# Four transformer layers in one kernel: the list scheduler orders the instructions by its other timing model

## The chip, the core and the metric

The kernel runs on one core of a Trainium2 chip. The metric is the device time of one execution in microseconds (us); lower is better. A core has five engines that run side by side, each through its own list of instructions in order, and that wait for one another through semaphores: TensorE (PE; its weight loads are shown as PEld), VectorE (DVE), ScalarE (ACT), GpSimd (POOL) and SyncE (SP), which here issues DMAs.

## The reference

The input `x` has 32 sequences of 64 tokens with 256 features; `ctx_2048`, of the same shape, is the context. Four layers follow one another, all in float32:

```python
x = L0(x, ctx, self_mask, cross_mask)  # self attention, cross attention, MLP (16 heads of 16)
x = L1(x, ctx)   # linear recurrence over the tokens: s = k*v + w*s per head, then a gated feed-forward
x = L2(x, ctx, ctx)  # two cross attentions with 16 heads of 128 and a bias key and value, then an MLP
x = L3(x, ctx, key_mask)  # cross attention (16 heads of 16) and an MLP
```

Every attention is `softmax(q k^T * scale) v`, every sublayer has a layer norm ahead of it and adds to its residual.

## The kernel before

The 2048 tokens are cut into four groups (`g` = 0 to 3) of 512 tokens, eight sequences each. Activations lie feature by feature as 128x512 tiles, two for 256 features. A layer of a group is a Python generator (`layer0` to `layer3`) that yields between steps, and `weave` interleaves a main generator with lighter ones at fixed rates: while layer 2 of group 0 is written, layer 1 of group 1 and layer 0 of group 2 are written between its steps, and so on. `keep` is a further light one: it computes the keys and values of layer 2's first attention ahead (tiles `k2p_f`, `v2p_f`, evicted to `fk` on ScalarE, L928, and `fv` on VectorE, L937), stores them in DRAM and loads them again later (`kd`, `vd`).

This text order isn't the order that the engines run. When the `TileContext` closes, a list scheduler takes all instructions with their dependencies and goes through them by a timing model: whatever the model holds ready, with the earliest place in the text first, is put next on its engine. The semaphores are set for that order. Buffers rotate within pools (`ps1`, four PSUM banks for single tiles; `ps2`, two pairs of banks), and an instruction that fills a buffer waits for the last reader of what was there.

Names that the rest uses:

- `norm` (L174 to L194): statistics and `xn` (L180) on VectorE, transposes `nt` on TensorE (L190), then `y` or `h`, feature by feature: half 0 on VectorE (L192), half 1 on ScalarE (L194).
- `linear` (L165): 128x512 matmuls, two for each output tile; `q2p`, `k2p`, `qp`, `kp`, `h` (the MLPs) and others. `token_linear` (L328): 128x256 matmuls, tiles `al`.
- `attn16`, the attention of layers 0 and 3: scores `sp` (L269, 32 rows of the array), softmax on VectorE and ScalarE, the product with the reciprocal sum on GpSimd (L276), transposes `tp` (L286), value products `pv` (L295), `oT` (L299).
- `bias_attn`, the attention of layer 2: scores `s2p` (L788, 64 columns of the array), softmax, transposes `tp2` (L802), value products `pv2` (L817, shown as `pv`), evictions `o` (L827 on ScalarE, L828 on VectorE), then `al_o`.
- the recurrence of layer 1, `states`: `vj` on TensorE (L550), a product (L559) and two scans (L565) on VectorE, a product on GpSimd (L566), `op` (L588) on TensorE.

The value products of layer 2 write two banks, one for each sequence of a pair (`b2`), and go through them in turn; `half` are rows of the array, `rows` its columns:

```python
for m in range(2):
    rows = slice(64 * m, 64 * m + 64)
    hc = (2 * pp + h2) * P + 64 * m
    for b2 in range(2):
        half = slice(64 * b2, 64 * b2 + 64)
        PE.matmul(
            pv[b2][rows, to : to + S], vals[bp][half, hc : hc + 64],
            pt[half, bp, h2 * S : (h2 + 1) * S], start=True, stop=True,
        )
```

Of the kernel before, what the change touches and what calls it, by code (L numbers as in the profile page):

```python
# [1072 lines left out]
def build(arrays):  # L1073
    import concourse.bacc as bacc

    nc = bacc.Bacc("TRN2", target_bir_lowering=False, num_devices=1)
    args = [
        nc.dram_tensor(f"in_{n}", a.shape, mybir.dt.from_np(a.dtype), kind="ExternalInput").ap()
        for n, a in arrays.items()
    ]  # L1080
    args.append(nc.dram_tensor("out_0", (P, G, TT, D), F32, kind="ExternalOutput").ap())
    with tile.TileContext(nc) as tc:
        kernel(tc, *args)
    return nc

# [12 lines left out]
```

## Time and profile before

| | before |
|---|---|
| median of 3 runs (lowest to highest) | 2216.41 us (2216.34 to 2218.59) |
| the profiled execution | 2216.37 us, span 2214.6 us |
| PE busy | 2057.4 us, 93% of the span |
| DVE busy | 1097.3 us, 50% |
| ACT busy | 632.9 us, 29% |
| POOL busy | 597.5 us, 27% |
| DMA | 197.25 MB, mean 89 GB/s |

The span is the time from the first to the last instruction that the hardware profiler recorded. Busy is the time in which an engine had at least one instruction running. A float32 matmul has two records in the trace, a transpose one. Tile names are shown without their numbers. "x <- y" in a list of waits means that x stood still until y was done. Clock is the share of TensorE's full clock that was granted.

### The profile page before, as it was taken

How to read it: one execution, taken by the hardware profiler on the slowest of the kernel's cores; microseconds unless marked ns; L12 is line 12 of the kernel's file. 1: busy time of each engine (PE TensorE's matmuls, PEld its weight loads, DVE VectorE, ACT ScalarE, POOL GpSimd, SP SyncE). 2: the span in 40 equal slices, each digit the busy share in tenths (PEclk: the TensorE clock that was granted, in tenths of full speed). 3: DMA queues.
4: the chain of work that ended last, by engine and by line, in shares of the span. 5: the costliest groups of instructions: out<-in, count | busy, mean ns of one | idle time of the engine just before them, and what ended most of it. 6: DMA issues, size and time to landing. Idle time of an engine off the chain costs nothing. (4 is left out here: it accounts for less than half of the span.)

```text
span 2214.6 us, 36273 instructions
## 1 busy us (share of the span) xinstructions
PE 2057.4 (93%) x15264; PEld 1242.9 (56%) x15264; DVE 1097.3 (50%) x1885; ACT 632.9 (29%) x1000; POOL 597.5 (27%) x498
## 2 busy tenths in 40 slices
PE   5889998899999898999997999999999999999998
PEld 3445444354555465755554656555566767565665
DVE  3552557423655636335556463266564355424661
ACT  1222322132321322232313132322233233222442
POOL 2331344213423314214324141233221112200220
PEclk9999998999999999999998999999999999999999
DMA  7233231226412212243121123341213342213010
GB/s 247 93 106 118 93 110 57 93 101 229 141 49 64 66 41 63 92 132 109 55 62 58 42 79 96 121 134 44 86 45 108 100 152 69 78 51 94 22 41 20
DMA packets 79794, 197.25 MB, mean 89 GB/s; under 512 B 9616, under 2 KB 14352, under 8 KB 79632
## 3 DMA queue, kind: packets, MB, share of 16 engines
q1 hardware_dynamic: 77472, 191.88, 27.1%
q8 instruction: 121, 1.98, 0.4%
q0 software_dynamic: 576, 2.10, 0.3%
q10 hardware_dynamic: 1584, 0.95, 0.2%
q14 instruction: 41, 0.34, 0.1%
HBM read 158.98 MB, written 35.91 MB: 88 GB/s over the span
## 5 line engine op out<-in xcount | busy, mean ns | idle before, releaser
L165 PE MATMUL q2p<-h,w 128*128 128x512 f32 x512 | 245.4, 612 | 6.8 <-DMA w<-in_wts 3.2
L328 PE MATMUL al_o<-w,o 128*128 128x256 f32 x1024 | 235.1, 388 | 11.7 <-DVE o L828 10.7
L328 PEld LDWEIGHTS al_o<-w,o 128*128 128x128 f32 x1024 | 196.6, 194 | 52.6 <-issue 20.6
L778 ACT ACTIVATE q<-q2p,vt 128x512 f32<-128x512 f32 x128 | 87.5, 685 | 278.9 <-PE q2p L165 275.7
L165 PEld LDWEIGHTS q2p<-h,w 128*128 128x128 f32 x512 | 94.9, 193 | 123.6 <-issue 105.5
L796 POOL TENSOR_TENSOR pn<-s,sm 128x512 f32<-128x512 f32 x64 | 69.7, 1091 | 285.2 <-DVE sm L209 198.2
L165 PE MATMUL k2p_f<-c,w 128*128 128x512 f32 x256 | 131.2, 634 | 4.9 <-DMA w<-in_wts 2.8
L726 PE MATMUL v2p_f<-w,c 128*128 128x512 f32 x256 | 122.4, 601 | 0.0
L165 PE MATMUL k2p<-c,w 128*128 128x512 f32 x256 | 120.7, 597 | 0.0
L726 PE MATMUL v2p<-w,c 128*128 128x512 f32 x256 | 119.1, 609 | 1.1 <-DVE k L764 1.1
L566 POOL TENSOR_TENSOR a<-a,r 128x1024 f32<-128x1024 f32 x32 | 76.1, 2378 | 109.8 <-DVE a L565 96.4
L937 DVE TENSOR_TENSOR fv<-v2p_f,vb 128x512 f32<-128x512 f32 x64 | 43.9, 687 | 124.7 <-PE v2p_f L726 124.7
L928 ACT ACTIVATE fk<-k2p_f,vt 128x512 f32<-128x512 f32 x64 | 43.9, 686 | 175.4 <-PE k2p_f L165 146.8
L341 DVE TENSOR_TENSOR x<-al_o,x 128x512 f32<-128x512 f32 x64 | 43.6, 683 | 101.2 <-PE al_o L328 101.2
L828 DVE TENSOR_SCALAR o<-pv,vt 128x256 f32<-128x256 f32 x128 | 55.8, 473 | 76.6 <-PE pv L817 76.4
L764 DVE TENSOR_SCALAR k<-k2p,vt 128x512 f32<-128x512 f32 x64 | 47.4, 743 | 91.4 <-PE k2p L165 91.4
L788 PEld LDWEIGHTS s2p<-k,q 128*64 128x64 f32 x2048 | 67.7, 138 | 40.8 <-issue 29.7
L817 PEld LDWEIGHTS pv<-pt,v 64*64 64x64 f32 x4096 | 72.8, 140 | 26.6 <-issue 18.4
L565 DVE TENSOR_TENSOR_SCAN a<-ws,a 128x512 f32<-128x512 f32 x64 | 85.4, 1368 | 1.7
L726 PEld LDWEIGHTS v2p_f<-w,c 128*128 128x128 f32 x256 | 49.6, 195 | 63.5 <-issue 61.3
L817 PE MATMUL pv<-pt,v 64*64 64x64 f32 x4096 | 81.7, 226 | 3.2 <-issue 1.5
L165 PEld LDWEIGHTS k2p<-c,w 128*128 128x128 f32 x256 | 49.4, 193 | 62.1 <-issue 59.4
(305 smaller groups left out, 3678.5 us busy)
## 6 DMA issues: line engine op xcount, KB each, us to landing
w<-in_wts SPq DMA_DIRECT2D x200, 512.0 KB, 3.7
kd<-fk SPq DMA_DIRECT2D x64, 260.0 KB, 2.1
k<-kd SPq DMA_DIRECT2D x64, 260.0 KB, 3.8
vd<-fv SPq DMA_DIRECT2D x64, 256.0 KB, 2.0
v<-vd SPq DMA_DIRECT2D x64, 256.0 KB, 4.5
vb<-in_vrow SPq DMA_DIRECT2D x20, 256.0 KB, 4.1
vs<-in_vrow SPq DMA_DIRECT2D x20, 256.0 KB, 3.4
c<-in_cT POOLq DMA_DIRECT2D x4, 512.0 KB, 11.6
```

Of the source, the lines that this page charges most:

```text
L165: PE.matmul(ps, w[:, o : o + cols], y[:, kc, :], start=(kc == 0), stop=(kc == NC - 1))
L328: PE.matmul(ps[:, a, :], y[kc][:, i * P : (i + 1) * P], wk[:, o : o + D], start=(kc == 0), stop=(kc == k - 1),)
L565: V.tensor_tensor_scan(a[:, i, :], ws[:, c, :], a[:, i, :], 0.0, ALU.mult, ALU.add)
L566: PL.tensor_tensor(a, a, r[:, c : c + 1, :].to_broadcast([P, 2, GT]), ALU.mult)
L726: PE.matmul(ps, cs[g][:, kc, bp * P : (bp + 1) * P], wv[:, 512 * kc : 512 * kc + 512], start=(kc == 0), stop=(kc == NC - 1),)
L764: V.tensor_scalar_add(k[:, :, :S], bt(ps), vec(f"L2_xattn_bk{a}", hd))
L778: A.activation(q, ps, AF.Identity, bias=vec(f"L2_xattn_bq{a}", hd))
L788: PE.matmul(sp[64 * h2 : 64 * h2 + 64, b // 4, (b % 4) * (S + 1) : (b % 4 + 1) * (S + 1)], qs[h2][:, b * S : (b + 1) * S], ks[h2][:, b, :] ...
L796: PL.tensor_tensor(pn, s[:, :, :S], rc.unsqueeze(2).to_broadcast([P, GB, S]), ALU.mult)
L817: PE.matmul(pv[b2][rows, to : to + S], vals[bp][half, hc : hc + 64], pt[half, bp, h2 * S : (h2 + 1) * S], start=True, stop=True,)
L828: V.tensor_scalar_add(ov[:, :, 1, :], src[1], bv)
L928: A.activation(k[:, :, :S], bt(ps), AF.Identity, bias=vec("L2_xattn_bk1", hd))
```

## The change

The context that holds the scheduler is opened with an option: the scheduler takes a timing model that follows queues and semaphores in place of its default one. Nothing in the text of the kernel changes, so the engines get the same instructions with the same operands, in another order, with semaphores set for it.

```diff
@@ -1079,7 +1079,7 @@
     args.append(nc.dram_tensor("out_0", (P, G, TT, D), F32, kind="ExternalOutput").ap())
-    with tile.TileContext(nc) as tc:
+    with tile.TileContext(nc, schedule_with_timeline_sim=True) as tc:
         tile_layers_kernel(tc, *args)
     return nc
```

## The prediction

> **What bounds the kernel now.** I read the page's busy rows first, then its slices, the waits, the timeline of single places, and last the instruction orders of the two built programs side by side.
>
> ```profile
> span 2214.6 us, 36273 instructions
> PE 2057.4 (93%) x15264; PEld 1242.9 (56%) x15264; DVE 1097.3 (50%) x1885; ACT 632.9 (29%) x1000; POOL 597.5 (27%) x498
> PE   5889998899999898999997999999999999999998
> PEclk9999998999999999999998999999999999999999
> ```
>
> TensorE is the bound: 2057.4 of 2214.6 us, so all idle time together is 157.2 us. A reordering can gain at most that, and it can lose in two ways: new idle time, or TensorE instructions that take longer beside other neighbours. Where the idle time sits is in the waits:
>
> ```profile
> PE tp_a L286 <- POOL s_a L276: 20.4, 6, 5.9
> PE nt_a L190 <- DVE xn_a L180: 19.8, 1, 19.8
> PE tp_b L286 <- POOL s_b L276: 13.9, 6, 7.1
> PE al_o L328 <- DVE o L828: 10.7, 5, 3.2
> PE sp_a L269 <- DVE s L205: 10.4, 4, 4.7
> ...
> PE tp_b L286 <- DVE fv L937: 5.5, 1, 5.5
> ```
>
> The columns are total us, times, longest. The 19.8 is the start, before any data is there. The rest are short waits in which an attention of layer 0 or 2 follows its softmax chain through VectorE and GpSimd.
>
> **What moves.** Each engine has the same instructions in both programs: 8112 matmuls, 1885 on VectorE. TensorE's are shifted by 4.1 places in the mean, VectorE's by 1.2, SyncE's DMAs by 0.3. So this is no new plan, but many small swaps. I price the TensorE swaps, then the stalls, then the rest.
>
> **1. The value products (pv, L817), +17.7 us.** One group is 32 matmuls of 64x64 into two PSUM banks (`b2`); the two banks use the two row halves of the array, `m` its two column halves. The source alternates them, and in the program of before 130 neighbouring pairs within the groups stay in one bank; in the changed one 736 do: it starts bank 0 with 8 or 9 matmuls, then bank 1, and alternates only after that. The trace of before has both patterns:
>
> ```profile
> 572.75 1.16 PE L817 MATMUL pv<-pt,v 64*64 64x64 f32 x64
> 573.84 1.13 PE L480 MATMUL mp<-t,w 32*128 32x512 f32 x4
> 574.89 3.70 PE L165 MATMUL q2p<-h,w 128*128 128x512 f32 x8
> 578.52 1.16 PE L817 MATMUL pv<-pt,v 64*64 64x64 f32 x64
> ...
> 1935.56 1.15 PE L788 MATMUL s2p<-k,q 128*64 128x65 f32 x32
> 1936.64 1.98 PE L165 MATMUL h_j<-y_j,w 128*128 128x512 f32 x4
> 1938.56 1.15 PE L788 MATMUL s2p<-k,q 128*64 128x65 f32 x32
> ...
> 1943.61 1.15 PE L817 MATMUL pv<-pt,v 64*64 64x64 f32 x32
> 1945.44 1.15 PE L817 MATMUL pv<-pt,v 64*64 64x64 f32 x32 [0.68 <-ACT hm_j L349]
> ```
>
> Each row is start, duration, and a count of records; a matmul of this type has two. Alternating, 64 records take 1.16 us; at 1943.61 one bank alone takes 1.15 us for 32. Take off the last record's own 0.218 us (median of the pv rows): 0.94/64 = 14.7 ns a record against 0.93/32 = 29.1, hence 14.6 ns more, 29.2 ns a matmul. 736 - 130 = 606 pairs x 29.2 ns = 17.7 us. Bounds: zero where bank 1 is really still held (then before would have waited), and 26.5 if the whole group at 788 is the price (it took 2.38 us with 28 such pairs: 1.22/28 = 44 ns, of which 0.14 is a wait). Sixty of the 64 groups of before show no wait inside, so I take 17.7.
>
> **2. Visits of small matmuls between long ones, +14 us.** Going from a 128-row, 128-column matmul (transposes apart) to one on a part of the array happens 124 times before and 180 times after, the way back 135 and 188: 54 more visits. Splits such as one score matmul (s2p, L788) ahead of q2p and the other 15 behind it make them. The rows above price one: eight records of q2p take 578.52 - 574.89 = 3.63 us to the next start, four of h_j between two small groups 1938.56 - 1936.64 = 1.92, and 3.63 - 1.92 = 1.71 for four more; so a visit costs the long ones 0.21. The small group pays its own start: the 32 s2p records hold TensorE for 1936.64 - 1935.56 = 1.08 us, while (1.15 - 0.225)/31 = 29.8 ns a record in the midst of the run (0.225 is the mean of one in the page) makes 0.95; 0.13 more. Ends 54 x 0.21 = 11 and 54 x 0.34 = 18; I take 14, nearer the first, since some visits only move. [...]
>
> **3. The stalls, -5 us, the least certain term.** Where the order around a wait is the same, it stays: tp_a at 772 and 1208 (5.9 each), sp_a at 749 and 1183 (4.5 and 4.7), the last nt_j (3.8), the start. At the start two VectorE instructions that wait for mc move behind the first norm, but the next instruction, k2p_f, waits for its weight until 24.8 us anyway: nothing. What can go is the stage where layer 1 of group 0 runs beside the cross attention of group 1:
>
> ```profile
> 280.00:320.00 40.00, 38.41 (x247) 19.91 (x246) 18.77 (x34) 12.22 (x19) 17.43 (x19) 1.00 0.33 108
> 320.00:360.00 40.00, 37.72 (x204) 17.52 (x206) 29.38 (x35) 8.98 (x17) 15.38 (x13) 0.91 0.19 68
> 360.00:400.00 40.00, 26.36 (x161) 13.30 (x154) 34.72 (x33) 8.94 (x14) 24.11 (x14) 0.83 0.14 50
> ```
>
> (Windows by stage: length, then busy PE, PEld, DVE, ACT, POOL, granted clock, DMA share, GB/s.) From 320 to 400 TensorE idles 2.3 + 13.6 = 15.9 us while VectorE is full, and from 280 to 320 VectorE is half empty. The changed order brings the state products (vj, L550) and their VectorE work (L559 1.20 us, two scans L565 of 1.37: 3.9 us a state) of four states forward. But it puts them ahead of the norm's xn_b (L180) and y_b (L192), on which qp_b and all of that attention wait: 14.5 us of state work now stands in front of y_b on VectorE that stood behind it. So a wait of up to some 11 us (14.5 less the 3.6 us state that ran there anyhow) opens at 318 for up to 15.9 that closes later. The middle of +11 and -15.9 is -2.5; the late stretch also runs at a granted clock of 0.83, which on its 26.4 busy us is 0.17 x 26.4 = 4.5 more to win, so I take -7. Elsewhere: al_o behind its evictions at 604 and 1039 (3.2 and 3.1) gets 8 and 6 more matmuls in front, -4; tp_a at 57 (5.8) gets 16 score matmuls in front, -1.5. New or longer: al_d behind og (2.7 twice) loses 1.4 us of cover twice, op behind its state 1 us twice, q2p behind h at 1554 3.0: +7.8. Sum -4.7.
>
> **4. The rest, nothing.** ScalarE gets 57 table loads for 64; at 1.283 us a row that is 9.0 us of an engine that is 29% busy, and no TensorE wait above 2.7 us ends on ScalarE: 0, bounds 0 and -9.0. [...] On SyncE's queue the latest-moved loads are k for s2p_110 behind eight others; before, these were all issued by 550.4 and s2p needs k at 567.6, with 4 us from issue to landing: hidden by 13 us; without that cover it would cost the 4 us.
>
> **Sum.** 17.7 + 14 = 31.7 us more on TensorE; it idles 7% of the time and part falls into waits that are there, so I count nine tenths, 28.5. Less 5: +23.5. The profiled execution took 2216.37 us (span 2214.6 and 1.8 around it), the median of the runs is 2216.41, so the two can be used alike: 2239.9, forecast 2240.
>
> **Rivals.**
> *A, faster: the stalls close.* Mechanism: the new order takes VectorE's state work out of the full stretch 360 to 400. It decides if y_b is not held up at 318: then -15.9 - 4.5 there, -5.5 for al_o and tp_a, and the products' bank order costs nothing because bank 1 is still held; against 14 for visits: 2216 - 26 + 14 = 2204. For it speaks the half-empty VectorE at 280 to 320; against it the order on VectorE and the pv rows without waits. 0.18.
> *B, much slower: VectorE blocks.* State work now also stands ahead of pv evictions (L828: 3.9 us at 602 and 1037, 7.6 at 1464) and of y_b (up to 11). If VectorE runs these first, TensorE waits at al_o and qp_b: 11 + 3.9 + 3.9 + 7.6 = 26 on top of 28.5: 2271. Against it: these state products come earlier on TensorE too. 0.19.
> *C, no difference.* The timing model changes little, mean shift 4 places; gains of A's 26 meet the 28.5: 2218. Against it the 606 pairs, whose price is measured. 0.08.
>
> **Chances.** The forecast has 0.55. Under 0.2% (4.4 us) this kernel's measurement cannot tell from none. Faster 0.18 (A), same 0.08 (C), slower 0.74 (forecast and B). The range leaves out the lower half of A and the upper half of B, one in ten on each side: 2208 to 2268.
>
> **What would show it.** Right: PE busy near 2085 to 2090; pv rows in the timeline with 1.4 to 1.5 us a group for 1.16; PE idle about 150. Step 2 is wrong if PE busy rises by no more than pv's share, step 3 if a wait of nt_b or qp_b on DVE at 318 is missing or the 360 to 400 stretch still has 13 us idle. The forecast as a whole is wrong if PE busy stays at 2057 or if idle falls below 125.

## The result and the profile after

The changed kernel takes 2290.31 us (median of 4 runs, 2286.05 to 2292.28) beside 2216.38 us before: the ratio is 1.033, 95% interval 1.031 to 1.035. The forecast was 2240, its range ended at 2268. The side was right, the size was not: +74 us for +23.5.

The page of the changed kernel, its span and busy row:

```profile
span 2288.5 us, 36279 instructions
...
PE 2105.9 (92%) x15264; PEld 1268.5 (55%) x15264; DVE 1114.6 (49%) x1885; ACT 624.4 (27%) x993; POOL 600.8 (26%) x498
```

The span grew by 73.9 us: TensorE is busy 48.5 us longer and idles 25.4 us longer (182.6 for 157.2). Of the busy time a part is clock. The clock records of the trace know two values, 1.0 and 0.5; laid over TensorE's busy time, 108.9 us ran at half clock before and 145.1 after. At half clock the work goes half as fast (records of 128x512 matmuls start 0.85 us apart at 1558 us of the kernel before and 0.43 us apart at 1561, when the clock is full again), so half of the difference, 18.1 us, is put down as time lost. So 73.9 = 25.4 idle + 18.1 half clock + 30.4 that is left, TensorE's work that takes longer at the same clock; runs 1 and 2 show what makes most of it. Terms 1 and 2 of the prediction, 31.7 together, meant the last number. Term 3, -5, meant the first two, 43.5.

The waits of TensorE in the changed kernel (total, times, longest, in us):

```profile
PE tp_a L286 <- POOL s_a L276: 14.0, 6, 6.0
...
PE al_d L328 <- POOL og L619: 9.5, 2, 4.7
PE qp_b L165 <- issue: 9.3, 1, 9.3
PE al_o L328 <- DVE o L828: 9.2, 3, 4.5
...
PE tp L802 <- POOL pn L796: 6.8, 3, 3.4
```

Some of the old waits did get shorter: tp_a 20.4 to 14.0, tp_b 13.9 to 7.4. In their place stand waits that the list of before hardly has or doesn't have: qp_b, nt_b (8.8 us in all), a longer al_d, tp behind pn, dwp behind xm on GpSimd (4.2 us). The largest are in the stage that the prediction priced at -7 (windows as before: length, busy PE, PEld, DVE, ACT, POOL, clock, DMA share, GB/s):

```profile
320.00:360.00 40.00, 24.71 (x77) 11.66 (x76) 28.05 (x29) 5.52 (x11) 16.24 (x10) 0.79 0.20 66
360.00:400.00 40.00, 31.85 (x197) 14.71 (x195) 29.93 (x31) 9.93 (x16) 20.00 (x12) 0.87 0.12 44
```

From 320 to 400 TensorE idles 15.3 + 8.1 = 23.4 us, where it idled 15.9 before. These are equal windows of time, not equal work. The instructions that the kernel before ran from 281.7 to 400 us run here from 285.3 to 423.8, 20.2 us longer: the idle time in them rises from 17.5 to 34.3 us, the busy time at half clock from 14.9 to 23.2. VectorE's timeline there shows why (start, duration):

```profile
323.63 6.66 DVE L565 TENSOR_TENSOR_SCAN a<-ws,a 128x512 f32<-128x512 f32 x4
330.21 3.38 DVE L180 TENSOR_SCALAR xn_b<-x,mv_b,rs_b 128x256 f32<-128x256 f32 x4
...
336.35 6.66 DVE L565 TENSOR_TENSOR_SCAN a<-ws,a 128x512 f32<-128x512 f32 x4
342.93 0.78 DVE L192 TENSOR_SCALAR y_b<-nt_b,vt 128x512 f32<-128x512 f32 x1
```

And TensorE's:

```profile
330.74 0.66 PE L190 MATMUL nt_b<-ct,xn_b 128*128 128x128 f32 x2 [4.43 <-DVE xn_b L180]
...
343.81 3.57 PE L165 MATMUL qp_b<-y_b,w 128*128 128x512 f32 x4 [9.26 <-issue]
347.22 1.88 PE L165 MATMUL kp_b<-c,w 128*128 128x512 f32 x4
```

Two states (two scans L565 each) stand in front of xn_b and two more in front of y_b. The three waits, 4.43, 1.60 (in the row that is left out) and 9.26, make 15.3 us, where the prediction had "up to some 11". The list calls the longest one "issue"; the start of qp_b at 343.81, right behind the end of y_b at 343.71, tells who it waited for. Its four records then take 3.57 us, at half clock up to 347.1; kp_b's four behind it take 1.88.

TensorE's own work in the changed kernel, with a cut score group and a group of value products:

```profile
597.90 0.33 PE L788 MATMUL s2p<-k,q 128*64 128x65 f32 x2
598.16 1.13 PE L480 MATMUL mp<-t,w 32*128 32x512 f32 x4
599.22 1.15 PE L788 MATMUL s2p<-k,q 128*64 128x65 f32 x30
...
604.37 1.55 PE L817 MATMUL pv<-pt,v 64*64 64x64 f32 x64
```

One score matmul goes ahead of mp and the other 15 follow it; a value group takes 1.55 us for 1.16.

### The profile page after: what moved, and what is told of

Same layout as the page of the kernel before. It is cut to its first block, busy times and chain, and to the rows that moved or that the text cites. A ratio compares the mean times of both kernels' runs of the same rounds, so it can differ in the third digit from the quotient of the medians.

```text
span 2288.5 us, 36279 instructions
## 1 busy us (share of the span) xinstructions
PE 2105.9 (92%) x15264; PEld 1268.5 (55%) x15264; DVE 1114.6 (49%) x1885; ACT 624.4 (27%) x993; POOL 600.8 (26%) x498
## 5 line engine op out<-in xcount | busy, mean ns | idle before, releaser
L566 POOL TENSOR_TENSOR a<-a,r 128x1024 f32<-128x1024 f32 x32 | 76.8, 2400 | 120.7 <-DVE a L565 97.9
L817 PEld LDWEIGHTS pv<-pt,v 64*64 64x64 f32 x4096 | 87.7, 138 | 28.0 <-issue 21.8
L817 PE MATMUL pv<-pt,v 64*64 64x64 f32 x4096 | 96.7, 226 | 3.4 <-issue 1.5
L200 DVE TENSOR_REDUCE mx<-s2p 128x8 f32<-128x520 f32 x64 | 44.2, 691 | 107.0 <-PE s2p L788 106.4
L828 DVE TENSOR_SCALAR o<-pv,vt 128x256 f32<-128x256 f32 x128 | 55.2, 473 | 79.7 <-PE pv L817 79.4
L565 DVE TENSOR_TENSOR_SCAN a<-ws,a 128x512 f32<-128x512 f32 x64 | 91.6, 1474 | 1.5
L788 PE MATMUL s2p<-k,q 128*64 128x65 f32 x2048 | 86.0, 226 | 3.2 <-DVE xm L482 1.3
```

What stands on the lines that cost most here:

```text
L200: V.tensor_reduce(mx, src, AX.X, ALU.max)
L565: V.tensor_tensor_scan(a[:, i, :], ws[:, c, :], a[:, i, :], 0.0, ALU.mult, ALU.add)
L566: PL.tensor_tensor(a, a, r[:, c : c + 1, :].to_broadcast([P, 2, GT]), ALU.mult)
L788: PE.matmul(sp[64 * h2 : 64 * h2 + 64, b // 4, (b % 4) * (S + 1) : (b % 4 + 1) * (S + 1)], qs[h2][:, b * S : (b + 1) * S], ks[h2][:, b, :] ...
L817: PE.matmul(pv[b2][rows, to : to + S], vals[bp][half, hc : hc + 64], pt[half, bp, h2 * S : (h2 + 1) * S], start=True, stop=True,)
L828: V.tensor_scalar_add(ov[:, :, 1, :], src[1], bv)
```

## The experiments

In each kernel below every engine's order is written out: at the end of the program text a chain of dependencies without semaphores ties each instruction to the one that shall stand ahead of it on its engine. With the orders of the changed kernel so pinned, single pieces of them can be put back. Diffs show the order of one engine's list. The measured change against the changed kernel is the difference of the two ratios to the kernel before, times 2216.4 us; a ratio's interval is about 0.0015 to 0.002 (4 us) to each side, so that of a difference is some 5 us. Gains of 4 to 6 us (runs 3, 4, 9, 10) are thus at the limit of what the times alone can tell, and lean on the traces. The pinned orders were not run without any edit; up to its edit kernel 4 is 1.5 us behind the changed one (at 556 us), and kernel 9 is 0.9 us ahead (at 630).

### 1. The value products in turn

```diff
-L817 pv_100_0_0 x9, then pv_100_0_1 x9, then in turn
+L817 pv_100_0_0, pv_100_0_1, pv_100_0_0, pv_100_0_1, ...
```

> The changed kernel with the order of every engine held, except that the 32 value products (L817) of each group alternate between their two PSUM banks as in the kernel before: 736 same-bank neighbours become 130. Theory 1 (the order of the banks has its own price on TensorE, 29 ns a pair): TensorE busy falls from 2105.9 to about 2089, the pv rows go back from 96.7 to about 82 us, and the time falls by 16 to 18 us, to 2272 to 2275. Rival (one bank was really held by its eviction, so the alternate order only turns work into a wait): TensorE idles more by the same amount, and the time stays within 5 us of 2290.

Measured: 2277.43 us, ratio 1.0279 (1.0263 to 1.0295), 11.5 us less than the changed kernel, where theory 1 had 16 to 18. The groups of TensorE, of the changed kernel:

```profile
L817 PE MATMUL pv<-pt,v 64*64 64x64 f32 x4096 | 96.7, 226 | 3.4 <-issue 1.5 <-DVE o L828 0.8 <-DVE vb L254 0.8
...
L269 PE MATMUL sp_i<-kb_i,qT_i 32*64 32x128 f32 x512 | 24.7, 303 | 2.1 <-DVE s_i L668 2.1
```

and of this one:

```profile
L817 PE MATMUL pv<-pt,v 64*64 64x64 f32 x4096 | 82.4, 223 | 5.1 <-ACT o L827 1.7 <-issue 1.5 <-DVE vb L254 0.8
```

The pv row (busy us, mean ns, idle) falls by 14.3 us, and its idle time rises by only 1.7: the second bank was hardly held. The order has a price of its own, 14.3 us / 606 = 24 ns a pair by the row. The rival is out. The bank and the row half of the array change together in these products, so the run doesn't tell which of the two sets the price.

### 2. Score groups together

```diff
-L269 sp_a_00 x6
 L242 vp_a_0 x4, vp_a_1 x4; L165 k2p_f x2; L726 v2p_f x2
-L269 sp_a_00 x10
+L269 sp_a_00 x16
```

> The changed kernel with every order held, except that groups of small score matmuls (L269, L788) that stood in two pieces around a long matmul are put together: visits of small matmuls between long ones fall from 180 to 141 (and the ways back from 188 to 150). Theory (a visit costs 0.21 to 0.34 us of TensorE): 39 fewer make 8 to 13 us, 2277 to 2282. Rival (visits are free, all of the loss is in waits and the clock): within 4 us of 2290, or slower where a group that is together waits for its last operand.

Measured: 2272.42 us, ratio 1.025 (1.023 to 1.0271), 18 us less. The scores sp_i, whose row in the changed kernel stands above:

```profile
L269 PE MATMUL sp_i<-kb_i,qT_i 32*64 32x128 f32 x512 | 17.9, 283 | 2.2 <-DVE s_i L668 2.2
```

The row falls by 6.8 us, that of s2p by 7.2 (86.0 to 78.8). It is more than expected (8 to 13 us), because I had counted visits of small matmuls between 128-row ones. Counted as cuts inside a score group there are 19 before and 79 after, and this kernel takes out 67, some of them between one small shape and another (as at 597.90 above). 18 / 67 = 0.27 us a cut lies between the 0.21 and 0.34 of the prediction's rows. TensorE's busy time falls by more than the time does:

```profile
PE 2078.2 (91%) x15264; PEld 1259.2 (55%) x15264; DVE 1114.5 (49%) x1885; ACT 624.4 (27%) x993; POOL 601.3 (26%) x498
```

That is 27.7 us less, and 10.8 us of it come back as idle time (193.4 for 182.6). So part of the work that is taken away does fall into waits.

### 3. One stage as before

```diff
 (TensorE's instructions up to 281 us of the kernel before: changed order)
-(281 to 549 us: changed order, all engines)
+(281 to 549 us: order of the kernel before, all engines)
 (all behind it: changed order)
```

> The changed kernel with one stage (281 to 549 us of the kernel before, TensorE's long stage where layer 1 of group 0 runs beside the cross attention of group 1) in the order of the kernel before on all engines; everything ahead of it and behind it in the changed order. Theory (state work on VectorE ahead of y_b opens waits of 9.3 us at qp_b and some 6 at nt_b, and the stage costs 10 to 20 us in all): the wait of qp_b at 343 goes, and the time falls by 10 to 20 us, to 2270 to 2280. Rival (the waits in this stage only take the place of those that stood between 360 and 400, as the record of the stage's end suggests: behind by 8.8 us at its start and by 18.8 at its end): a fall of at most 10, of which some 5 are the value products and visits that are inside the stage.

Measured: 2283.45 us, ratio 1.0304 (1.0288 to 1.032), 6 us less: the rival's size (at most 10), not the theory's (10 to 20). TensorE's idle time falls to 170.5 us, and the waits at 331 and 343 are gone, but most of that is given back inside the stage. When the same instructions are done, this kernel is ahead of the changed one by 20.9 us at 418 us and by 6.8 at 556.

### 4. GpSimd's xm first

```diff
-L796 pn_0
-L720 vb
 L487 xm_1 x2
+L796 pn_0
+L720 vb
```

> The changed kernel with every order held, except that in the stage around 570 us GpSimd gets the two masked copies xm (L487) ahead of the add at L720, as before; in the changed kernel that add waits 3.8 us for its DMA and xm, for which dwp (L165) waits, stands behind it. Theory 1 (this one order costs its own wait of 4.2 us and the half clock that follows it): the wait of dwp goes and the time falls by 8 to 12 us, to 2278 to 2282. Theory 2 (only the wait itself counts): 4 us, 2286. Rival (the next operand is late anyway): none.

GpSimd in the changed kernel:

```profile
572.91 1.26 POOL L720 TENSOR_TENSOR vb<-vb,vs 128x512 f32<-128x512 f32 x1 [3.80 <-DMA vs<-in_vrow]
574.13 4.64 POOL L487 TENSOR_TENSOR xm<-xm,y_d 128x1024 f32<-128x1024 f32 x2
```

Measured: 2284.96 us, ratio 1.0314 (1.0294 to 1.0333). That is 4 us less, within the two intervals. In the profiled executions the wait of dwp is gone from the list of longer ones, and this kernel goes from 1.5 us behind the changed one at 556 us to 7.2 ahead at 587, on the same instructions, and ends 7.8 ahead. But that execution (2282.57 us) was the fastest of the four. Its trace shows 8.7 us at this place, the size of theory 1; the four times have 4 us, that of theory 2, and with some 5 us to each side they don't rule out that it is worth nothing. How much this edit is worth stays open.

### 5 and 6. TensorE's order against that of the other engines

```diff
 PE: order of the kernel before   (6: of the changed kernel)
-DVE, ACT, POOL, SP: as in the kernel before   (6: as in the changed kernel)
+DVE, ACT, POOL, SP: ordered anew by the other timing model   (6: by the first one)
```

> TensorE's 8112 matmuls are held in the order of the kernel before, and the other timing model orders VectorE, ScalarE, GpSimd and SyncE around them. Theory 1 (what the change costs lies in the order of TensorE itself: the visits of small matmuls, the value products, and waits that come from where a matmul stands): 2216 to 2225, TensorE busy 2055 to 2062. Theory 2 (some 40 us, idle time and half clock, come from the order of VectorE and GpSimd): 2240 to 2260 with busy near 2060 to 2075 and idle near 185.

> The reverse: TensorE's matmuls are held in the order of the changed kernel, and the timing model of the kernel before orders the other four engines around them. Theory 1 (TensorE's order is the cause): 2280 to 2295, busy near 2100. Theory 2 (the order of the other engines is half of it): 2245 to 2260, with busy near 2090 and idle near 155.

Measured: 2227.01 us, ratio 1.0042 (1.0026 to 1.0057), with TensorE's old order; 2295.49 us, ratio 1.0355 (1.0342 to 1.0368), with its new one. TensorE is busy 2071.5 us in 5 and 2113.4 in 6. Of the waits of 6:

```profile
PE al_o L328 <- DVE o L828: 10.2, 5, 4.5
...
PE qp_b L165 <- issue: 6.3, 1, 6.3
```

Theory 1 holds, though each time lies a little above its range (2216 to 2225, 2280 to 2295); theory 2's are far off. The loss goes with TensorE's order. The waits of qp_b and al_o stand there too when the first timing model orders VectorE: TensorE asks for the states earlier and VectorE's list follows (in 6 two states, and the product L559 of two more, stand between xn_b, at 327.69 us, and y_b, at 342.14). Number 5 has a lesson of its own: its TensorE order is that of before and it idles 154.9 us for 157.2, yet it is 9 us slower. TensorE's busy time at half clock is 134.9 us for 108.9: 13 us lost in the clock, with waits of nearly the same sum at other places.

### 7. Four repairs at once

Edit: those of 1, 2, 3 and 4 together.

> The changed kernel with four repairs at once: the value products in turn, split score groups put together, the stage of 281 to 549 us as before, and GpSimd's xm first. Alone these gave 2277.4, 2272.4, 2283.5 and 2285.0 for 2290.3. Theory (they are independent): 13 + 18 + 7 + 5 = 43 less, some 2247, TensorE busy near 2065 to 2075. Rival (work taken from TensorE turns into waits that are already there, as idle rose from 183 to 193 when the scores were put together): half to two thirds of it, 2261 to 2269.

Measured: 2246.2 us, ratio 1.0129 (1.0114 to 1.0144), 45 us less than the changed kernel; the four alone gave 11.5 + 18 + 6 + 4 = 39.5. Within the intervals they add up. TensorE is busy 2058.5 us, as before; what is left is idle time, 180.2 us. On the same instructions this kernel is 2.4 us ahead of the kernel before at 1306 us and ends 24 us behind: what is left comes behind 1306.

### 8. The kernel before, with the same two repairs of TensorE's work

```diff
-L269 sp_a_01 x5
 L502 wp_0, wp_1
-L269 sp_a_01 x11
+L269 sp_a_01 x16
```

> The kernel before with every order held, but its 14 split score groups put together (visits 124 to 118) and its last 130 same-bank neighbours of the value products put in turn. Theory (both cost TensorE time in the kernel before too): 14 split groups x 0.46 us (18 us for 40 of them in the changed kernel) = 6.4, and 130 pairs x 19 ns (11.5 us for 606) = 2.5: 2207 to 2212, faster. Rival (before, the pieces stood where TensorE had to wait anyway, and the bank that comes second is held by its eviction): 2214 to 2220.

Measured: 2218.26 us, ratio 1.0005 (0.9995 to 1.0015). TensorE is busy 2049.4 us, 8.0 less, and idles 166.6, 9.4 more. Here the rival holds: work taken away only made TensorE wait longer for the next operand. The scores sp_a that now stand together wait 3.7 us for 11.3, and the transposes tp_a behind them 31.4 us for 20.4.

### 9. Evictions ahead of the states

```diff
+L828 o_110 x2
 L559 a_1 (a03)
 L565 a_1 (a03) x2
-L828 o_110 x2
```

> The changed kernel with one thing moved on VectorE: in layers 1, 2 and 3 the two first evictions of the value products (L828, o200 and o201) stand ahead of the state work (L559, L565 of a03, or a00 to a01 in layer 3) again, as in the kernel before; 18 places on VectorE change and none on the other engines. Theory (rival B of the prediction: state work ahead of the evictions holds al_o): the waits of al_o at 639 and 1074 (4.5 us each) and at 1508 (3.5) fall to under 1 us, 12 us of idle time go, and the half clock that follows each (6.8, 6.8 and 3.4 us) goes with it, up to 8 us more: 2272 to 2280. Rival (the state then is late by as much for op L588 and vj L550): idle stays within 4 us of 183 and the time above 2284.

(Its layers 1, 2 and 3 are layer 1 of the groups 1, 2 and 3, at some 640, 1070 and 1510 us.)

Measured: 2284.32 us, ratio 1.0303 (1.0288 to 1.0319), 6 us less. The waits of TensorE from 630 to 716 us in the changed kernel, and from 630 to 710 in this one:

```profile
PE al_o L328 <- issue: 4.5, 1, 4.5
...
PE op L588 <- POOL a L566: 2.1, 2, 1.1
```

```profile
PE op L588 <- POOL a L566: 4.2, 3, 2.1
...
PE al_o L328 <- DVE o L828: 0.6, 1, 0.6
```

The wait of al_o went from 4.5 to 0.6 us, and op waits 2.1 us longer for the state that now comes later. On the same instructions this kernel was 7.9 us ahead of the changed one at 644 us, for 0.9 ahead of the edit, and had 1.8 left at 706. At the second place it gained 4.9 and kept it; at the third it gained 3.2 by 1510 and had given back 4.5 at 1514. So the theory holds in one place and the rival in two.

### 10. xn_b and y_b ahead of the states

```diff
+L177 rs_b; L576 ruk x2; L180 xn_b x4
 L559 a_0 (a00), a_0 (a01)
-L177 rs_b; L576 ruk x2
 L565 a_0 (a00) x2
+L192 y_b
 L565 a_0 (a01) x2
-L180 xn_b x4
 ...
-L192 y_b
```

> The changed kernel with one thing moved on VectorE: in the stage around 320 to 345 us the norm's xn_b1 (L180) and y_b1 (L192) stand ahead of the states a01, a02 and a03 (L559, L565) where they stood behind; 21 places on VectorE change. Theory (VectorE's order alone opened these waits): nt_b1's 4.4 and 1.6 and qp_b1's 9.3 us fall to under 3 us together, and of these 12 us some 6 to 10 stay as a gain: 2280 to 2284. Rival (the stage is full of VectorE work in any order, so the states are then waited for at op or vj, and the whole stage as before gained only 7): 2286 to 2292.

Measured: 2284.99 us, ratio 1.0307 (1.0291 to 1.0323), 5 us less. TensorE, in this kernel:

```profile
332.88 1.95 PE L165 MATMUL qp_b<-y_b,w 128*128 128x512 f32 x4 [0.84 <-ACT y_b L194]
...
349.60 1.12 PE L269 MATMUL sp_b<-kb_b,qT_b 32*64 32x128 f32 x12 [6.18 <-DVE kb_b L233]
```

qp_b starts 10.9 us earlier, and the next product of the same attention, sp_b, waits 6.2 us for kb_b, which stands behind two states of its own. On the same instructions this kernel was 3.1 us behind the changed one at 318, ahead of the edit, 11.9 us ahead at 346 and 4.5 at 358. So VectorE's order does open the wait, and of the 15.0 us that the edit won there half only moves on.

### 11 and 13. The better stretch of the changed order, in the kernel before

```diff
 (order of the kernel before, with the two repairs of number 8)
-(749 to 1306 us: order of the kernel before)
+(749 to 1306 us: changed order; score groups together, value products in turn)
 (order of the kernel before, with the two repairs of number 8)
```

and in 13 also, within that stretch, on VectorE:

```diff
+L828 o_111 x2
 L559 a_2 (a03)
 L565 a_2 (a03) x2
-L828 o_111 x2
```

> The kernel before with only the stretch from 749 to 1306 us (TensorE's instructions 2040 to 4301) in the changed order on all engines, its split score groups put together and its value products in turn. With the four repairs the changed order was behind by 16.5 us at the start of this stretch and ahead by 2.5 at its end. Theory (the changed order contains a stretch that is better by itself): 12 to 19 us less than before, 2198 to 2205. Rival (the gain there is the clock's recovery, or waits carried in from the earlier part): 2212 to 2220.

> The kernel before with the stretch of 749 to 1306 us from the changed order (as in the run that gave 2204.6), and within it, on VectorE, the two evictions o200 and o201 (L828) of layer 2 ahead of the state a03 (L559, L565) again: 5 places on VectorE. In the trace of 2204.6 that stretch fell back by 5.1 us between 1010 and 1038; in the changed kernel the same edit kept 4.6 us there. Theory: another 3 to 5 us, 2199.5 to 2202. Rival (the state a03 is then late for op or vj, as in layer 1, where 5.8 of 7.6 us were given back): 2203 to 2206.

Measured: 2204.57 us, ratio 0.9947 (0.9933 to 0.9961), and 2198.87 us, ratio 0.9921 (0.9907 to 0.9935). Both are faster than the kernel before and the changed one. The repairs outside the stretch aren't the cause: number 8, which has them alone, took 1.0005, and on the same instructions kernel 11 is 1.7 us behind the kernel before at 749 us, 12.1 ahead at 1306 and 12.4 at 2200. The busy row of 13, whose span is 2198.6 us:

```profile
PE 2046.9 (93%) x15264; PEld 1236.6 (56%) x15264; DVE 1102.3 (50%) x1885; ACT 632.5 (29%) x1000; POOL 604.6 (27%) x498
```

The changed order contains a stretch that is better by itself: the waits of sp_a and tp_a, which the prediction had said would stay, fall in it from 9.8 to 6.7 and from 13.0 to 10.7 us. It was hidden by what the order lost elsewhere: the changed kernel is 41.1 us behind at 749 us and 33.5 at 1306.

### 12. Only the first half changed

```diff
 (up to TensorE's instruction 4301, 1306 us before: changed order)
-(behind it: changed order)
+(behind it: order of the kernel before)
```

> The changed kernel up to TensorE's instruction 4301 (1306 us of the kernel before), and from there on the order of the kernel before on all engines. In the traces the changed kernel is behind by 35.4 us at that point and by 74 at the end. Theory (each half of the loss belongs to the order of its own half): 2250 to 2256. Rival 1 (the loss of the first half is carried into waits that were there anyway, and part of it is made good): 2235 to 2247. Rival 2 (the second half is slow because of what it inherits, a clock or queues behind, and not by its own order): 2270 to 2290.

Measured: 2248.85 us, ratio 1.0143 (1.0127 to 1.0158). So 32 us of the loss belong to the first half and 42 to the second, close to the 35 and 39 by the traces, and neither half makes the other's good. The window of the second half, of the kernel before:

```profile
1306.00:2214.60 908.60, 879.44 (x7194) 564.82 (x7191) 433.86 (x783) 281.19 (x440) 187.12 (x156) 0.99 0.26 79
```

and of the same instructions in the changed one:

```profile
1341.40:2288.50 947.10, 903.00 (x7164) 577.81 (x7164) 435.98 (x785) 273.11 (x432) 187.68 (x157) 0.97 0.25 76
```

In the second half TensorE is busy 23.6 us longer and idles 44.1 for 29.2 us; 42.4 us of its busy time are at half clock for 16.4, so 13 of the 23.6 are clock. The prediction's sum has one wait of that half, q2p behind h at 1554, +3.0; q2p's waits for h are 2.2 us in all, for 2.6 before.

## Why the prediction was off

**Term 1, +17.7: right mechanism, a third too large.** Run 1 gives 11.5 us, the row 14.3: 24 ns a pair for 29. (0.2 us of it is a slip: 29.1 less 14.7 is 14.4 ns a record, not 14.6, and the term 17.5.)

**Term 2, +14: right price, count a little low.** 60 more cuts of score groups at the 0.27 us of run 2 make 16. Together with term 1, 31.7 stood for the 30.4 us that the two traces leave. The side of the forecast comes from these two terms; by term 3 alone the kernel would have been faster.

**Term 3, -5: this step failed.** It was +25.4 us of idle time, and +18.1 of clock, 43.5 together. The prediction took waits that close and waits that open as about equal, and the clock as a gain.

- The stage of the three windows (280 to 400 us) was put at -7. I took the middle between a new wait of up to 11 and a closing one of 15.9. On the same instructions it was +16.8 us of idle time and +4.2 of clock. The new waits were 15.3 us: the scans of the four states took 13.3 us by their two rows for some 10 at 1.2 us each. The work of the old stretch (361.5 to 400 us before, 385.0 to 423.8 after) idles 11.0 us for 13.6, so it gave back 2.6, because pv_b waits anew in it (4.7), and sp_b ahead of it (5.1). In this stage a wait on a full VectorE didn't close because some of its work went earlier: runs 3 and 10 show that it moved to the next product.
- al_o was put at -4, for the matmuls that came in front of it. Its row has 6.3 us more idle time (18.0 for 11.7). At the three places of run 9, where states stand ahead of L828, its longer waits are 12.5 us for 8.8. The prediction had this as rival B, and run 9 shows the mechanism; I gave it 0.19 because the states come earlier on TensorE too. That didn't help: at 633.28 us of the changed kernel a state's product (1.18 us) and two scans (3.43) run on VectorE ahead of L828, and al_o waits 4.5. The rest is another wait, which the prediction didn't have: 4.3 us at 1878 us, where the eviction L827 on ScalarE comes late, behind an exponential of layer 3 (L206).
- Not foreseen at all: xm behind an add that waits for a DMA on GpSimd (4.2 us at dwp), tp behind pn (6.8 for 1.6), the halves of the clock. al_d (+2.8 said, +4.0 measured) was about right. tp_a's and tp_b's gains, 13 us together, were larger than the 1.5 said for tp_a.
- The clock had entered once, as a gain of 4.5 us in the stage. It went with most of the long waits (18 of the 25 over 2.5 us): in the changed kernel the idle time rose by 25 us, and the clock added 18 to it.

The prediction's own signs for step 3 didn't catch this. The wait at qp_b was there and the window from 360 to 400 idled less than 13 us, as step 3 wanted; what failed was the balance of the two.

**The nine tenths.** A share of the added work was to fall into existing waits. Run 1 shows nothing of the kind (13.9 us less busy, 0.8 more idle), run 2 shows 10.8 of 27.7 us, and in the kernel before run 8 shows all of it. It is no fixed share; it seems to depend on whether the instruction behind is waiting already.

**Rival B** had the right places (y_b, and al_o at three places) and, with its 2271, the nearest number. Its 26 us of waits aren't what undoing them returns: runs 9 and 10 gave 6 and 5.

Part of it stays open: the runs give single edits for some 45 us of the 74. What is left lies behind 1306 us, mainly as idle time and half clock. Run 12 shows that the order there is the cause, and runs 5 and 6 that it goes with TensorE's. The traces show two places: between 1460 and 1540 us of the kernel before the changed one falls 9.5 us further behind (its al_o waits 3.5 us for L828), and between 1820 and 1860 10 us (al_o waits 4.3 us for L827, and tp 3.4 for pn). That these waits make the loss is not shown: run 9 undid part of the first and gave back there what it had won, and no run undid the others.

## What to carry to other kernels

A reordering that leaves the bound engine's work alone can still make that work longer, by cutting groups of small matmuls (0.27 us a cut in run 2) and by breaking an alternation (24 ns a pair in run 1), and both can be counted in the two orders and priced from rows of the old trace. Stalls couldn't be priced like that here: in an order that was balanced, be ready for it that moved work on a second engine delays whoever it is put ahead of (9.26 us at qp_b), that a closed wait reopens at the next operand (6.18 us at sp_b in run 10), and that new waits cost their length and more in the clock (here 25.4 us of idle time, and 18.1 lost at half clock). If a new order loses, compare the two stretch by stretch before throwing it away: here one stretch of it, put into the old order, gave 0.8%.

## What the runs showed of the hardware

**Most long waits of TensorE came with a piece of half clock.** Of the 25 waits of over 2.5 us in the changed kernel 18 have a piece of half clock that begins between their start and 3.5 us behind their end; before, 14 of 19. But for the last, which the end of the program cuts, the low pieces are whole multiples of 3.4 us (3.4, 6.8, 10.2, 13.7, 17.1 in the changed kernel). What starts a piece the traces don't show: at 1557 us of the kernel before a half-clock piece of 3.4 us begins, and in the 13.6 us ahead of it TensorE idled 2.0 in all.

**The same VectorE instruction took up to six times as long beside GpSimd.** VectorE's 1885 instructions kept it busy for 1114.6 us, 1097.3 before. Of that the 64 scans (L565) have 6.2 us, 91.6 for 85.4. A scan with no GpSimd instruction beside it takes 1.21 us (the mean of 41 in the changed kernel); beside GpSimd's L566 one takes up to 3.30 (at 326.99). The second of the four xn_b took 2.43 us for 0.4: it began at 330.52, when GpSimd's product had just begun,

```profile
330.44 2.36 POOL L566 TENSOR_TENSOR a<-a,r 128x1024 f32<-128x1024 f32 x1 [0.15 <-DVE a L565]
```

and ended at 332.95, 0.15 us behind its end. All ten xn (L180) of the changed kernel that took over 1 us (1.13 to 2.45) began 0.08 to 0.16 us behind the start of a GpSimd instruction and ended 0.15 or 0.16 behind its end. Not every VectorE instruction took longer: L192 takes 0.80 us in the mean beside GpSimd (19 in the changed kernel) and without (21). What makes the difference the traces don't show. By these times the price of putting a state ahead of xn_b was the state, and also GpSimd's product that the state sets off: 2 us at this place, which no sum of VectorE's rows contains.
